# A planned graph-network kernel: the block product in two more groups, paired reciprocals, and another order of the work

## The chip, the cores and the metric

The kernel runs on one core of a Trainium2 chip. TensorE (PE) multiplies matrices and transposes, VectorE (DVE), ScalarE (ACT) and GpSimd (POOL) work on elements, and SyncE (SP) issues most transfers. All engines run side by side and wait for each other through semaphores. The metric is the device time of one execution in microseconds. Matmul results go to PSUM, which has eight banks of 128 x 512 float32; everything else is kept in SBUF. All arithmetic is float32.

## The reference

`x` is (128, 64, 256): 128 graphs of 64 nodes with 256 features; `adj` is (128, 64, 64). Four layers follow each other, each as `x = layernorm(x + layer(x, adj))`:

```python
# layer 0: gated graph network, five steps, A = (adj != 0)
for l in range(5):
    m = h @ weight[l]
    agg = einsum('bij,bid->bjd', A, m)
    h = gru_cell(agg, h, w_ih, w_hh, b_ih, b_hh)
# layer 1: graph isomorphism network, W1 is (256, 1024), W2 is (1024, 256)
agg = epsilon * x + adj @ x
h = silu(rmsnorm(agg @ W1 + b1))
out = h @ W2 + b2
# layer 2: hyperbolic: logmap0, adj @ x, expmap0, project
# layer 3: graph attention
h = x @ W_w.T + W_b
u = adj * exp(e[:, None] + f[None, :] + a_b)     # e = h @ a1, f = h @ a2
out = (u / sum(u)) @ h
```

## The kernel before

**Tiling.** Two graphs share the 128 partitions as one block, with a block-diagonal adjacency tile of 128 x 128. There are 64 blocks. Four blocks make a group (`NB` = 4, 512 rows), so there are 16 groups, numbered 0 to 15. `group(g)` records all the work of one group: loads of `x` and `adj`, five recurrent steps (`gated`), layer 0's residual and normalisation, layer 1 (`by_sums` or `as_it_is`, then the second product `ps_o`), layer 2 (`ps_sup`), layer 3 (`ps_a`, `ps_att`) and the store. Buffers are taken in three sets, by `g % 3`.

**Seven products for eight.** A product of a 2 x 2 block matrix with another needs eight block products. The kernel uses a scheme of seven (Winograd's variant of Strassen's), with sums of the weights' blocks made once at the start and sums of the activations' blocks made by DVE. The recurrent products (lines 755 and 761, PSUM tiles `p_r`, `p_u`, `p_v`, `p_w`, `p_hx`, `p_ix` and so on) use it in all groups. Layer 1's first product uses it in groups 0 to 13 (`by_sums`, PSUM tiles `p_1h`, `p_uh`, `p_vh`, `p_wh`: 28 matmuls of 256 columns, ten additions on DVE at line 947). Groups 14 and 15 use `as_it_is`: 16 plain matmuls of 512 columns into `ps_hid`, with W1 loaded a second time for this.

**Normalisation.** Groups 0 to 13 (`summed`) take row sums and squares as by-products of DVE's residual addition (line 653) and of an ACT pass; groups 14 and 15 use DVE's own statistics instructions (lines 674, 675). The power -0.5 is on POOL (line 678).

**The order.** No engine's order is written out by hand. Every helper (`pe`, `dve`, `act`, `pool`, `copied` ...) only records an operation with an assumed cost; each group is one stream. `Flow.issue` then plans: it keeps a clock for each engine and time and again picks, among the next operations of up to `WINDOW` = 4 streams, the one that can start first. Ties and ranks are settled by a rule, which changes every `STRETCH` us of the plan as a digit of `CHOICES` says: 0 is the earliest stream first, 1 puts the latest stream first and transfers by stream, higher digits compare the length of the work still behind an operation, with a lag from stream to stream (`LAGS`). `copied` and `scaled` may go to ACT or DVE, as the planner finds. The operations are emitted in the planned order, and each engine executes exactly that order: an instruction whose input is late holds up everything behind it on its engine.

**Denominators.** In layer 3 a matmul per block gives 256 features and, in one more column, the denominator. DVE multiplies (line 1113), takes the reciprocal (line 1114), multiplies again (line 1115) and adds the residual (line 653), block by block.

Of the kernel before, what the change touches and what calls it, by code (L numbers as in the profile page):

```python
# [128 lines left out]
class Flow:  # L129
# [23 lines left out]
    WINDOW, STRETCH, LAGS = 4, 4.0, (60.0, 150.0)  # L153
    CHOICES = ("0001210202220220200202001001011000011111001011100001101010000011101000001000101020011100002211002111"
               "0010002212011101012212212100222012102200120001000200200012010111210112220000000202201121220010001010"
               "0101010111011100020120010000001100000000010010010020012002000010100022210001100000200000220210100100"
               "0011110100100021120110001101100200002101000000100001000011010111011010100010010010200102001101000100"
               "2011010001000100000011000010101102000012100000100020221100000001000010001100000000100102112000002011"
               "0021000010011011100111000000100100110100022111011111110001100101110110110000111000011000")
# [81 lines left out]
def kernel(  # L241
# [41 lines left out]
    NG = B // G  # L283
    NBLK = B // 2
    NF = 3
# [59 lines left out]
    x_rows = x.rearrange("(g b t) n d -> g (t n) b d", b=NB, t=2)  # L345
    out_rows = out.rearrange("(g b t) n d -> g (t n) b d", b=NB, t=2)
    adj_blocks = adj.rearrange("(g b t) i j -> g t i b j", b=NB, t=2)
# [13 lines left out]
    loads, plain = {}, []  # L361

    def load(g):
        s = g % NF
        xt = unit("B", s, f"x_{g}", (P, NB, D))
        flow.op("SP", 0.5, lambda: nc.sync.dma_start(xt.tile(), x_rows[g]), [xt], kb=512)
        for t in range(2):
            q = quads[t]
            flow.op("SP", 0.75, lambda q=q, t=t: nc.sync.dma_start(edge[s][q, :, q], adj_blocks[g, t]),
                    [(edge[s], t)], kb=64)  # L370
        loads[g] = xt
# [226 lines left out]
    def group(g):  # L598
        s = g % NF

# [4 lines left out]
        def u(tag, name, shape=(P, R)):  # L605
            return unit(tag, s, f"{name}_{g}", shape, bufs(tag))
# [7 lines left out]
        def feats_of(dst, src, n):  # L614

            ps = bank("ps_T")
            for j in range(2):
                for c in range(KD):
                    turn(lambda j=j, c=c: nc.tensor.transpose(
                        ps[:, c * HR + j * P:c * HR + (j + 1) * P], src[:, 2 * n + j, c * P:(c + 1) * P], ident.tile()),  # L620
                        [ps], [(src, 2 * n + j)])
            copied(512, lambda: dst[:, :, half(n)], lambda: blocks_of(ps.tile()), [(dst, n)], [ps])

        def rows_of(src, n):

            ps = bank("ps_hr")
            for j in range(2):
                for c in range(KD):
                    turn(lambda j=j, c=c: nc.tensor.transpose(  # L629
                        ps[:, j * D + c * P:j * D + (c + 1) * P],  # L630
                        src[:, c, (2 * n + j) * P:(2 * n + j + 1) * P], ident.tile()), [ps], [(src, n)])
            return ps

        def aggregate(dst, src, b0, n):

            ps = bank("ps_agg")
            for j in range(2):
                for c in range(KD):
                    pe(128, lambda j=j, c=c: matmul(
                        ps[:, c * HR + j * P:c * HR + (j + 1) * P], src[:, b0 + j, c * P:(c + 1) * P],  # L640
                        ed[:, 2 * n + j, :], 0, 1), [ps], [(src, b0 + j), ed])
            copied(512, lambda: dst[:, :, half(n)], lambda: blocks_of(ps.tile()), [(dst, n)], [ps])
            return ps
# [14 lines left out]
        def layer_norm(y, st, tag, name, norm=None):  # L658
# [5 lines left out]
            if summed:  # L664
                dve(4, lambda: nc.vector.tensor_scalar(mv[:, :, 0], st[:, :, 0], -1.0 / D, None, OP.mult), [mv], [st])  # L665
                for b in range(NB):
# [4 lines left out]
                    ve[:, :m, :], over(st[:, :, 1], m), 1.0 / D, eps2[:, :m, :], OP.mult, OP.add), [ve], [st])  # L671
            else:
                for b in range(NB):
# [3 lines left out]
                    ve[:, :m, :], over(mv[:, :, 1], m), eps2[:, :m, :], OP.add), [ve], [mv])  # L677
            pool(1.25, lambda: nc.gpsimd.tensor_tensor(rstd[:, :m, :], ve[:, :m, :], pow2[:, :m, :], OP.pow), [rstd], [ve])  # L678
# [12 lines left out]
        if g == NG - 2:  # L691


            for k in range(KD):
                w = unit("h", (NG - 3) % NF, f"w1_{k}", (P, H), 2)
                flow.op("SP", 0.5, lambda w=w, k=k: nc.sync.dma_start(w.tile(), w1k[:, k, :]), [w], kb=512)
                plain.append(w)
# [7 lines left out]
        copied(512, lambda: adjT.tile(), lambda ps=ps: tiles_of(ps.tile()), [adjT], [ps])  # L705
        for t in range(2):
            q = quads[t]
            dve(128, lambda q=q: nc.vector.tensor_scalar(ed[q, :, q], ed[q, :, q], 0.0, None, OP.not_equal),
# [6 lines left out]
        def gated(l, h):  # L715
# [5 lines left out]
            def agg_of(n):  # L721

                if l:
                    ps = rows_of(h, n)
                    copied(512, lambda: hr[:, 2 * n:2 * n + 2, :], lambda: blocks_of(ps.tile()),
                           [(hr, 2 * n), (hr, 2 * n + 1)], [ps])
                aggregate(agg, hr, 2 * n, n)
# [8 lines left out]
            def sums(x, i):  # L736
                t = t_of[i]
                dve(512, lambda: nc.vector.tensor_sub(t[:, :2, :], x[:, :, half(1)], blocks_of(x[:, 0, :])),  # L738
                    [(t, t1), (t, t3)], [x], True)
                dve(256, lambda: nc.vector.tensor_sub(t[:, t2, :], x[:, 1, half(1)], t[:, t1, :]),  # L740
                    [(t, t2)], [(x, 1), (t, t1)], True)
                dve(256, lambda: nc.vector.tensor_sub(t[:, t4, :], t[:, t2, :], x[:, 1, half(0)]),
# [8 lines left out]
            def gate(ps, m, v, first, last):  # L751

                for i, w in ((1, w_h), (0, w_a[l])):
                    for c in range(KD):
                        pe(256, lambda i=i, w=w, c=c: nc.tensor.matmul(  # L755
# [4 lines left out]
            def prod(ps, j, w, m, v, first=False):  # L760
                pe(256, lambda: nc.tensor.matmul(  # L761
# [3 lines left out]
            def onto(o, ps, j, x, w, r):  # L765
                dve(300, lambda: nc.vector.tensor_add(o(), ps[:, j * HR:(j + 1) * HR], x()), w, [ps, *r])

            def state_side():
# [11 lines left out]
                def biased(n, c, ps, j, x, r):  # L780
                    dve(300, lambda: nc.vector.scalar_tensor_tensor(  # L781
# [3 lines left out]
                copied(256, su, lambda: px[:, :HR], [(hs, 0)], [px])  # L785
                prod(px, 0, w_hn, m12, block(1, 0)[1])
                scaled(256, out(0, 0), lambda: px[:, :HR], lambda: 1.0, lambda: b(0), [(hnb, (0, 0))], [px, half_b])
# [17 lines left out]
            def plus(o, n, ps, x, m):  # L805
                dve(512, lambda: nc.vector.tensor_add(o[:, :, half(n)], blocks_of(ps.tile()), x[:, :, half(m)]), of(o, n), [ps, *of(x, m)])  # L806

            def tanh_half(c, o, src, i, w, r):
                act(256 if len(w) == 1 else 512, lambda: nc.scalar.activation(  # L809
                    o(), src(), AF.Tanh, bias=half_b[:, i * KD + c:i * KD + c + 1], scale=0.5), w, [*r, half_b], TANH)  # L810

            def times_state(n):
                dve(512, lambda: nc.vector.scalar_tensor_tensor(
# [3 lines left out]
            def input_side():  # L817
# [14 lines left out]
                onto(0, 1, lambda: px[:, HR:].unsqueeze(1), px)  # L832
                prod(py, 1, w_in[l], ms3, sum_of(t3)[0], True)
                prod(py, 0, w_in[l], ms1, sum_of(t1)[0])
                onto(3, 1, lambda: py[:, HR:].unsqueeze(1), py)
# [5 lines left out]
                onto(1, 2, lambda: blocks_of(py.tile()), py)  # L841
# [3 lines left out]
            copied(420, lambda: uu[:, :, half(1)], lambda: blocks_of(p1.tile()), of(uu, 1), [p1])  # L845
# [26 lines left out]
            for c in range(KD):  # L872
                act(512, lambda c=c: nc.scalar.activation(uu[:, c, :], uu[:, c, :], AF.Tanh, bias=bih(2 * KD + c)),
                    [*of(uu, 0, c), *of(uu, 1, c)], [*of(uu, 0, c), *of(uu, 1, c), cols], TANH)
            for n in range(2):
                v = half(n)
                dve(512, lambda v=v: nc.vector.tensor_sub(hN[:, :, v], h[:, :, v], uu[:, :, v]), [(hN, n)], [(h, n), *of(uu, n)], True)
                dve(512, lambda v=v: nc.vector.scalar_tensor_tensor(
                    hN[:, :, v], uz[:, :, v], 1.0, hN[:, :, v], OP.add, OP.mult), [(hN, n)], [(hN, n), *of(uz, n)], True)
                dve(512, lambda v=v: nc.vector.scalar_tensor_tensor(  # L880
# [275 lines left out]
```

## Time and profile before

| quantity | value |
|---|---|
| median of 3 runs | 2380.03 us (2379.65 to 2380.22) |
| profiled execution | 2378.74 us |
| its span, first to last instruction | 2376.8 us |
| granted TensorE clock in it | 0.994 |
| PE busy | 2329.7 us, 98% |
| weight loads (PEld) busy | 2039.0 us, 86% |
| DVE busy | 1892.0 us, 80% |
| ACT busy | 1247.2 us, 52% |
| POOL busy | 341.2 us, 14% |

The span runs from the first to the last instruction of the program; the execution's time is a little longer. PE and PEld overlap. A float32 matmul leaves two PE records in the trace. In the tables by stretch, "clock" is the share of full speed granted to TensorE. A wait "A <- B: total, times, longest" is idle time of A's engine that ended when B was done. The chain of work is followed back from the last instruction, at each step to what released it.

### The profile page before, as it was taken

Reading aid. Unit: us, or ns where it says so; the run is one execution under the profiler, and the core shown is the slowest. Engines: PE = TensorE matmul, PEld = TensorE weight load, DVE = VectorE, ACT = ScalarE, POOL = GpSimd, SP = SyncE. Lnnn points to the kernel's source line nnn. Section 1 sums busy time; section 2 is a strip of 40 time slices with the busy share of each in tenths; the row PEclk is TensorE's granted clock in tenths of the full one; section 3 lists DMA queues with packets and bytes.
Section 4 is the critical chain, followed back from the end, with each engine's and each line's share of the span. In section 5 each row is a group of like instructions: output and inputs, shape, how many; then the busy total and the mean of one; then the engine's idle time right before and its main releaser. Section 6 shows DMA issues by size and latency. Waiting matters only on the chain.

```text
span 2376.8 us, 32667 instructions
## 1 busy us (share of the span) xinstructions
PE 2329.7 (98%) x11938; PEld 2039.0 (86%) x11938; DVE 1892.0 (80%) x4293; ACT 1247.2 (52%) x2667; POOL 341.2 (14%) x272
## 2 busy tenths in 40 slices
PE   9999999999999999999999999999999999999995
PEld 8788888888888888888888888888888888888864
DVE  5688878878878878888787787878798787887865
ACT  3333455566445546465644655555465555545364
POOL 0300111411110200211101121201212120021011
PEclk9999999999999999999999999999999999999997
DMA  3000001000000000000000000000000000000000
GB/s 123 10 1 1 12 1 36 3 10 28 13 1 1 30 1 27 3 28 2 10 21 1 18 12 1 30 1 30 1 28 3 1 30 1 27 1 10 27 10 18
DMA packets 39729, 36.22 MB, mean 15 GB/s; under 512 B 9957, under 2 KB 38657, under 8 KB 39569
## 3 DMA queue, kind: packets, MB, share of 16 engines
q1 hardware_dynamic: 37840, 32.25, 4.3%
q8 instruction: 95, 1.56, 0.3%
q10 hardware_dynamic: 1328, 1.31, 0.2%
q0 software_dynamic: 400, 0.57, 0.1%
q14 instruction: 66, 0.53, 0.1%
HBM read 25.74 MB, written 8.39 MB: 14 GB/s over the span
## 4 chain that ended last, share of the span: by engine, by line
PE 93%; DVE 5%; ACT 1%; issue 1%; POOL 0%; POOLq 0%; ACTq 0%; DVEq 0%
PE p_v L755 11%; PE p_r L755 11%; PE p_w L755 11%; PE ps_o L313 9%; PE ps_agg L313 7%; PE p_hy L761 6%; PE p_u L755 6%; PE p_iy L761 6%; PE p_hx L761 4%; PE p_ix L761 4%; PE ps_hr L629 3%; PE ps_a L313 2%; PE p_vh L942 2%; PE p_wh L942 2%; PE p_1h L942 2%; PE ps_sup L313 1%
## 5 line engine op out<-in xcount | busy, mean ns | idle before, releaser
L678 POOL TENSOR_TENSOR rstd<-ve,pow 128x4 f32<-128x4 f32 (+1 forms) x64 | 78.9, 1233 | 1309.1 <-DVE ve L670 1192.2
L313 PE MATMUL ps_o<-w2s,hid 128*128 128x256 f32 x1024 | 230.9, 381 | 0.0
L313 PEld LDWEIGHTS ps_o<-w2s,hid 128*128 128x128 f32 x1024 | 194.7, 191 | 26.3
L755 PE MATMUL p_v<-tB,w_a 128*128 128x256 f32 x640 | 170.9, 380 | 0.0
L755 PE MATMUL p_v<-tA,w_h 128*128 128x256 f32 x640 | 170.3, 380 | 0.0
L755 PE MATMUL p_r<-hT,w_h 128*128 128x256 f32 x640 | 168.3, 381 | 0.0
L755 PE MATMUL p_r<-agg,w_a 128*128 128x256 f32 x640 | 167.3, 379 | 0.0
L809 ACT ACTIVATE U<-U,half_b 128x512 f32<-128x512 f32 (+1 forms) x160 | 95.2, 629 | 106.8 <-DVE U L806 106.7
L313 PEld LDWEIGHTS ps_agg<-edge,hr 128*128 128x128 f32 x1024 | 137.4, 192 | 7.9 <-issue 0.5
L313 PE MATMUL ps_agg<-edge,hr 128*128 128x128 f32 x1024 | 138.9, 275 | 0.0
L761 PE MATMUL p_iy<-tB,w_in 128*128 128x256 f32 x480 | 133.7, 380 | 0.6 <-DVE V L826 0.5
L755 PEld LDWEIGHTS p_v<-tB,w_a 128*128 128x128 f32 x640 | 120.7, 190 | 15.9
L755 PEld LDWEIGHTS p_r<-agg,w_a 128*128 128x128 f32 x640 | 120.0, 190 | 16.4 <-issue 1.0
L761 PE MATMUL p_hy<-tA,w_hn 128*128 128x256 f32 x480 | 132.1, 380 | 1.9 <-DVE tA L738 1.1
L781 DVE SCALAR_TENSOR_TENSOR hnb<-p_hy,half_b,hs 128x256 f32<-128x256 f32 x240 | 108.7, 478 | 31.6 <-PE p_hy L761 30.4
L331 ACT COPY agg<-ps_agg 128x512 f32<-128x512 f32 x148 | 86.0, 582 | 90.0 <-PE ps_agg L313 89.2
L755 PEld LDWEIGHTS p_v<-tA,w_h 128*128 128x128 f32 x640 | 119.1, 190 | 16.0 <-DVE U L806 0.8
L809 ACT ACTIVATE V<-V,half_b 128x256 f32<-128x256 f32 (+1 forms) x160 | 88.1, 586 | 76.6 <-DVE V L806 76.2
L331 ACT COPY hr<-ps_hr 128x512 f32<-128x512 f32 x122 | 70.8, 583 | 106.7 <-PE ps_hr L629 105.5
L755 PEld LDWEIGHTS p_r<-hT,w_h 128*128 128x128 f32 x640 | 114.6, 190 | 13.9 <-ACT V L331 0.4
L667 ACT ACTIVATE x_n<-y,mv 128x256 f32<-128x256 f32 x168 | 83.3, 498 | 58.8 <-DVE mv L665 58.7
L336 ACT ACTIVATE x_n<-y,off,rstd 128x256 f32<-128x256 f32 x160 | 84.0, 589 | 42.6 <-DVE off L682 42.6
(262 smaller groups left out, 5825.7 us busy)
## 6 DMA issues: line engine op xcount, KB each, us to landing
x<-in_x_dram SPq DMA_DIRECT2D x16, 512.0 KB, 3.5
xr<-in_x_dram SPq DMA_DIRECT2D x16, 512.0 KB, 3.5
out_dram<-x_n SPq DMA_DIRECT2D x16, 512.0 KB, 2.9
edge<-in_adj_dram SPq DMA_DIRECT2D x32, 64.0 KB, 2.3
wm<-in_L_gnn_weight_dram SPq DMA_DIRECT2D x5, 256.0 KB, 4.8
w2s<-in_L_gnn_W_dram SPq DMA_DIRECT2D x1, 1024.0 KB, 9.4
w<-in_L_gnn_W_dram SPq DMA_DIRECT2D x2, 512.0 KB, 3.4
w_in_L_gnn_w_hh_dram<-in_L_gnn_w_hh_dram ACTq DMA_DIRECT2D x1, 512.0 KB, 5.4
```

The lines of the kernel that those rows point to most:

```text
L313: return nc.tensor.matmul(o, lhsT, rhs, start=(k == 0), stop=(k == nk - 1))
L331: flow.either([("ACT", 0.22 + 0.00077 * n, lambda: nc.scalar.copy(o(), i())), ("DVE", 0.145 + 0.00105 * n, lambda: nc.vector.tensor_copy(o ...
L336: flow.either([("ACT", 0.3 + 0.0008 * n, lambda: nc.scalar.activation(o(), i(), AF.Identity, bias=bias(), scale=scale())), ("DVE", 0.145 + ...
L629: turn(lambda j=j, c=c: nc.tensor.transpose(ps[:, j * D + c * P:j * D + (c + 1) * P], src[:, c, (2 * n + j) * P:(2 * n + j + 1) * P], iden ...
L667: act(400, lambda b=b: nc.scalar.activation(o[:, b, :], y[:, b, :], AF.Square, bias=mv[:, b, 0:1], accum_out=st[:, b, 1:2]), [(o, b), (st, ...
L678: pool(1.25, lambda: nc.gpsimd.tensor_tensor(rstd[:, :m, :], ve[:, :m, :], pow2[:, :m, :], OP.pow), [rstd], [ve])
L755: pe(256, lambda i=i, w=w, c=c: nc.tensor.matmul(ps[:, c * HR:(c + 1) * HR], w[:, m, c * P:(c + 1) * P], v[i][0](), start=first and i == 1 ...
L761: pe(256, lambda: nc.tensor.matmul(ps[:, j * HR:(j + 1) * HR], w[:, m, :], v[0](), start=first, stop=True, skip_group_check=True), [ps], [ ...
L781: dve(300, lambda: nc.vector.scalar_tensor_tensor(out(n, c)(), ps[:, j * HR:(j + 1) * HR], b(c), x(), OP.add, OP.add), [(hnb, (n, c))], [p ...
L809: act(256 if len(w) == 1 else 512, lambda: nc.scalar.activation(o(), src(), AF.Tanh, bias=half_b[:, i * KD + c:i * KD + c + 1], scale=0.5) ...
L942: pe(256, lambda c=c: nc.tensor.matmul(ps[:, c * HR:(c + 1) * HR], w1f[:, w, (2 * q + c) * P:(2 * q + c + 1) * P], v[0](), start=first and ...
```

## The change

The grouping stays at four blocks and 16 groups; a list `SIZES` now holds the group sizes, and many lines are only rewritten in terms of it (`HB`, `HR`, `R`, `feats`, `in_rows`, `halves_of`, `blocks_in`), with the same shapes as before. Four things differ in what is executed:

- `as_it_is` and its loads of W1 are gone: groups 14 and 15 take `by_sums` like the others.
- Layer 3's denominators are done for two blocks at a time: both matmuls into two banks, then one reciprocal and one product for the pair.
- The planner has another list of choices, with stretches of 6 us and one rule more (lag 0).
- Some assumed costs that the planner uses are other numbers (a copy of 512 columns out of PSUM was costed as 420 in two places, for example). They alter the plan, not an instruction.

```diff
-    WINDOW, STRETCH, LAGS = 4, 4.0, (60.0, 150.0)
-    CHOICES = ("0001210202220220200202001001011000011111001011100001101010000011101000001000101020011100002211002111"
...
+    WINDOW, STRETCH, LAGS = 4, 6.0, (0.0, 60.0, 150.0)
+    CHOICES = ("0010000320333333330030000000030000303010330000003330300030300030300003033330301303000001103313000330"
...
-        if g == NG - 2:
-            for k in range(KD):
-                w = unit("h", (NG - 3) % NF, f"w1_{k}", (P, H), 2)
-                flow.op("SP", 0.5, lambda w=w, k=k: nc.sync.dma_start(w.tile(), w1k[:, k, :]), [w], kb=512)
-                plain.append(w)
...
-        def as_it_is():
-            for c in range(KH):
-                ps, (v, parts) = bank("ps_hid"), chunk(c)
-                for k in range(KD):
-                    pe(512, lambda ps=ps, k=k, c=c: matmul(
-                        ps.tile(), plain[k][:, c * P:(c + 1) * P], aggm[:, k, :], k, KD), [ps], [plain[k], aggm])
-                copied(512, lambda v=v: v, lambda ps=ps: ps.tile(), parts, [ps])
-                square(c)
-
-        as_it_is() if plain else by_sums()
+        by_sums()
...
-        for b in range(NB):
-            ps = bank("ps_att")
-            pe(256, lambda ps=ps, b=b: matmul(ps[:, :D + 1], adjT[:, b, :], hw[:, b, :D + 1], 0, 1), [ps], [adjT, (hw, b)])
-            dve(4, lambda ps=ps, b=b: nc.vector.tensor_mul(rd[:, b:b + 1], ps[:, D:D + 1], hw[:, b, D + 1:]), [(rd, b)], [ps, (hw, b)])
-            dve(4, lambda b=b: nc.vector.reciprocal(rd[:, b:b + 1], rd[:, b:b + 1]), [(rd, b)], [(rd, b)])
-            dve(4, lambda b=b: nc.vector.tensor_mul(rd[:, b:b + 1], rd[:, b:b + 1], hw[:, b, D + 1:]), [(rd, b)], [(rd, b), (hw, b)])
-            onto_rows(y3, b, st3, ps, 0, lambda b=b: rd[:, b:b + 1], x3, [(rd, b)])
+        for b0 in range(0, NB, 2):
+            att, two = [bank("ps_att") for _ in range(2)], slice(b0, b0 + 2)
+            for j, ps in enumerate(att):
+                b = b0 + j
+                pe(256, lambda ps=ps, b=b: matmul(ps[:, :D + 1], adjT[:, b, :], hw[:, b, :D + 1], 0, 1), [ps], [adjT, (hw, b)])
+                dve(4, lambda ps=ps, b=b: nc.vector.tensor_mul(rd[:, b:b + 1], ps[:, D:D + 1], hw[:, b, D + 1:]), [(rd, b)], [ps, (hw, b)])
+            parts = [(rd, b0), (rd, b0 + 1)]
+            dve(4, lambda two=two: nc.vector.reciprocal(rd[:, two], rd[:, two]), parts, parts)
+            dve(4, lambda two=two: nc.vector.tensor_mul(rd[:, two], rd[:, two], hw[:, two, D + 1]), parts, [*parts, (hw, b0), (hw, b0 + 1)])
+            for j, ps in enumerate(att):
+                b = b0 + j
+                onto_rows(y3, b, st3, ps, 0, lambda b=b: rd[:, b:b + 1], x3, [(rd, b)])
```

## The prediction

> **What bounds the kernel now.** I read the page's busy times and the shares of the chain first. They name the engine.
>
> ```profile
> PE 2329.7 (98%) x11938; PEld 2039.0 (86%) x11938; DVE 1892.0 (80%) x4293; ACT 1247.2 (52%) x2667; POOL 341.2 (14%) x272
> PE 93%; DVE 5%; ACT 1%; issue 1%; POOL 0%; POOLq 0%; ACTq 0%; DVEq 0%
> ```
>
> PE (TensorE) is busy for 98% of the span and holds 93% of the chain, so the time is PE's work plus PE's gaps. VectorE (DVE) at 80% is the next limit: it causes gaps wherever it falls behind. Next, the busy time by stretches of 60 us shows where PE is not full.
>
> ```profile
> 360.00:420.00 60.00, 58.74 (x315) 51.69 (x314) 53.17 (x123) 33.21 (x78) 7.14 (x4) 1.00 0.11 36
> 420.00:480.00 60.00, 57.34 (x292) 49.09 (x291) 51.85 (x80) 35.18 (x62) 25.30 (x18) 1.00 0.01 3
> ...
> 2220.00:2280.00 60.00, 57.04 (x263) 43.56 (x261) 51.66 (x106) 27.16 (x49) 6.04 (x4) 1.00 0.06 18
> 2280.00:2340.00 60.00, 51.44 (x200) 38.19 (x200) 32.56 (x97) 33.71 (x63) 7.36 (x6) 0.91 0.00 1
> 2340.00:2400.00 60.00, 14.37 (x65) 11.48 (x64) 25.03 (x99) 16.98 (x40) 6.74 (x5) 0.82 0.05 18
> ```
>
> The columns are stretch, length, then busy time of PE, PEld, DVE, ACT and POOL, and the granted clock. PE lacks 1.3 and 2.7 us in the two early rows, and 3.0, 8.6 and 22.4 (36.8 less 14.4) us in the last three. The two rows of the start lack 3.0 us and the 35 rows between 120 and 2220 us lack 10.1 us together; 26 of the 35 show no gap. So 34 of 47 idle us lie behind 2220 us, where only groups 14 and 15 are left. The waits of PE name the causes, and the chain gives the order of that end.
>
> ```profile
> PE ps_T L619 <- ACT x_n L336: 10.0, 1, 10.0
> PE ps_sup L313 <- ACT tan L1048: 5.9, 1, 5.9
> PE p_ix L761 <- DVE V L826: 3.3, 2, 2.6
> ...
> PE ps_ss L313 <- DVE sqt L930: 2.1, 1, 2.1
> ```
>
> ```profile
> 2262.99 5.15 PE ps_hid L313 x12
> ...
> 2303.41 25.48 PE ps_o L313 x118
> ...
> 2336.52 3.58 PE ps_sup L313 x8
> ...
> 2352.20 4.21 PE ps_a L313 x16
> ```
>
> The last recurrent product ends at 2262.8 us, the last ps_o at 2328.9, the span at 2376.8. So there are 66.1 us from the first to the second, and a tail of 47.9 us behind it in which the normalisations of two groups run on DVE, ACT and POOL and PE mostly waits.
>
> **Prices.** Two records make one fp32 matmul. ps_o gives 25.48 us / 59 = 0.432 us per 256 columns; ps_hid 5.15 / 6 = 0.858 per 512. Out of the same chain: a transpose 0.11, an aggregation matmul 0.222 (8 records 0.89), a ps_ss matmul 0.20.
>
> **Layer 1's first product in groups 14 and 15.** Before: 16 matmuls of 512 columns, 13.73 us. After: 28 of 256, 12.10 us. The difference is 1.63 us, 3.3 us for both. A rule of the Trainium skill speaks against this ("TensorE: Matmul & The Clock Gate", "Back-to-back issue gap"): in a stream of weight load and matmul the spacing is set by both, 81 ns at 128 columns, some 28 ns over the bare stream, and nothing extra at 512. With 28 ns on each of the four passes of an fp32 matmul (0.858 us for 512 columns is four times 512 at 2.4 GHz), 28 matmuls would pay 3.1 us and the edit would lose 1.5 us per group, 3.0 in all. The rows decide: 0.432 is half of 0.858 within 1%, with as many weight loads beside it as here. I take -3.3.
>
> On the other engines: ten additions out of PSUM per group come to DVE, which the first fourteen groups show at 0.688 us, and three differences (0.88, 0.49, 0.49), 8.7 us per group; ACT loses four copies of 0.58. These are not free: they lie where DVE paces PE. They are counted in the walk below. The two loads of W1 (512 KB, 3.4 us to landing) and their issues leave SP's queue; no wait of PE is on them, so 0.
>
> **Denominators by pairs.** Reciprocal and product (0.163 + 0.159 us) are issued 32 times in place of 64: 10.3 us less DVE. DVE has 485 us free, so under PE's work this is worth 0; in the tail one group's share, 0.65 us, is on the chain and is counted there. The cost: the first block of a pair waits for the second's matmul (0.43 us) and two banks are held; PE at 98% shows that banks are not short.
>
> **The end in the new order.** What I can read of the changed kernel is the order of instructions on each engine, not times. Group 13 is now held back: 24 of its 32 ps_o matmuls, and its layers 2 and 3, stand behind the last recurrent product. PE's work behind that point:
> before: 32 ps_hid 27.5, 8 transposes 0.9, 8 aggregations 1.8, ss 1.6, rms 0.9, 64 ps_o 27.6, 8 sup 3.5, 16 ps_T 1.8, 16 ps_a 7.0, 8 att 3.5 = 76.1 us;
> after: 24 ps_o 10.4, transposes 0.9, 16 aggregations 3.6, 56 products 24.2, ss 1.6, rms 0.9, 64 ps_o 27.6, 12 sup 5.2, 24 ps_T 2.6, 24 ps_a 10.4, 12 att 5.2 = 92.6 us.
> So 16.5 us move behind the point, and with the 3.3 saved, 19.8 us less lie ahead of it. The wait of 2.65 us at 2259 us (p_ix behind the state additions L826, because DVE does group statistics first) also goes: in the new order the additions of group 14 are interleaved with the other group's rows.
>
> How long does the new end take? I walk the listed orders with the rows' durations from the last recurrent product (0).
> (a) DVE ends group 14's state (4 x 0.7) between group 15's rows and its statistics (4 x 0.5), POOL's pow 1.1, ACT's x_n: first aggregation at 13.5, where PE has 11.2 us of work: 2.3 idle. Copies and the late x_n of group 14 cost about 1 more.
> (b) Products: DVE has some 24 us queued (20 additions of 0.69, six differences, 15 small ones of 0.17 for group 13, sums of squares 0.77). The squares of group 15 are summed at 39.5, PE got to 38.4. ss, ms, pow 1.16, rms, first product of DVE (0.74) and Silu with a table load (1.28 + 0.72): ps_o of group 15 starts at 48.4, idle 1.9.
> (c) 32 ps_o take 13.8; group 14's squares and rms come late by about 1 and 0.7; its ps_o starts at 64.8 and ends, with 33 matmuls left (14.3), at about 80. Idle in all about 9 against 6 before.
> (d) The tail. Tan of group 14 is ready after 7.7 (before: 7.6). Then three groups share DVE: from there on its list sums to 34.9 us (y 0.48 each, statistics 0.5 a block, small ones 0.17, two additions of wb 1.14). Two places queue: th of group 15 and 14 behind one Tanh table load (1.28), and the second half copy of group 14's x3T on ACT behind four squares of group 13 (2.8), which wait for DVE. The chain reaches the last att at 39.5, pow at 43.3, x_n at 44.7, and with the 4.3 us from last x_n to span end (2372.5 to 2376.8) I get 49. Before: 47.9.
> So the end takes 80 + 49 = 129 us against 114.0 before.
>
> Clock: behind idle stretches of 5.9 and 10.0 us the records of ps_sup and ps_a last 0.427 in place of 0.216 (clock 0.82 in the last row), about 3.6 us in all. The skill's rule (same page, "What's actually happening") is half clock after an idle window of about 3.4 us. The longest idle of the walk between two tail products is about 4.4, so by the rule the half clock can return: 129 would be 132. By the row it need not: the wait of 2.65 us at 2259 was followed by full speed. I take 129 and keep 132 in the range.
>
> **The body under a new order.** Start (3.0) and the gaps from 120 to 2220 us (10.1) depend on a planned order that cannot be timed from a listing. Below: 10.1 us less, all gone. Above: each of the 35 rows has the mean gap of the nine that show one (10.1 / 9 = 1.1), 39 us, 29 more. Nearest is the row itself, since the same work runs at the same DVE load: 0.
>
> **Sum.** 2262.8 - 19.8 - 2.7 + 129 = 2369.3 us of span, 7.5 less than 2376.8. The profiled execution took 2378.74, 1.9 more than its span; the median of the runs shown is 2380.03, 3.2 more than the span. Prediction 2369.3 + 3.2 = 2372.5, rounded 2372.
>
> **Rivals.**
> 1. The gain is eaten (within 0.2%). The DVE queue of three groups makes the tail 55 instead of 49: 2378. For it: DVE is the chain there and ACT waits behind it. Against: PE's idle tail has room.
> 2. Slower: the tighter order opens gaps in the body. Every PE instruction there waits in a fixed order for DVE, as p_ix and p_hy do now; in the recurrent stretches from 120 to 300 us DVE is at 81 to 85%. It decides for slower by 0.2% once body gaps pass 10.1 + 12.3 = 22.4 us, 0.64 per row of 60 us; at 0.8 per row the time is 2390. Against: 26 rows show none.
> 3. Clearly faster: the order closes the body's gaps and the waits of (a) to (c), 10.1 + 4: 2358. For it: the gaps are few and large, and one other order may miss all of them. Against: DVE's load in (b).
> 4. The product's saving doesn't appear, by the rule above: 3.0 lost in place of 3.3 saved, 2378.
>
> **How the numbers follow.** Forecast 0.5, rival 1 and 4 together 0.2, rival 2 0.1, rival 3 0.2. A measurement of this kernel tells about 0.2%, 4.8 us, from no change: faster means below 2375.3, slower above 2384.8. The forecast's own range, 2366 to 2378, lies four fifths below 2375.3: with rival 3 that makes 0.6, and as part of rivals 1 and 4 ends just below the bound, 0.68. Slower keeps 0.09, the rest is same. Range 2357 to 2382: it takes in rivals 1, 3 and 4 and the 3 us of half clock, and leaves rival 2 out.
>
> **What would show it.** p_1h to p_wh in the last two groups at 0.432 us each and no ps_hid; 32 reciprocals; 110 to 135 us from the last p_iy to the end with group 13's ps_att among the last products; the tail from the last ps_o at 46 to 53; idle PE between 120 and 2220 us of 5 to 15 us. The prediction is wrong if the body's idle time changes by more than 8 us, or if the tail, with DVE over 70% busy in it, is not near 49.

## The result and the profile after

The changed kernel takes 2366.73 us (median of 4 runs, 2364.33 to 2366.86) against 2379.84 us (2379.32 to 2380.22): ratio 0.9943, 95% interval 0.9925 to 0.9960, 13.1 us less. The profiled execution took 2366.68 us with a span of 2364.9 us; before it was 2378.74 and 2376.8. So the spans differ by 11.9 us.

Busy times and the shares of the chain, kernel after:

```profile
PE 2329.6 (99%) x11986; PEld 2046.1 (87%) x11986; DVE 1904.2 (81%) x4271; ACT 1236.0 (52%) x2643; POOL 340.1 (14%) x272
PE 91%; DVE 7%; ACT 1%; issue 1%; POOL 0%; POOLq 0%; ACTq 0%; DVEq 0%
```

PE is still the bound, and its busy time is the same within 0.1 us although its work is 3.3 us smaller by the prices of the prediction. So the 11.9 us are idle time. Busy time by stretches says where; the first two rows answer to the early rows shown of before, the others to its last three:

```profile
360.00:420.00 60.00, 60.00 (x302) 52.76 (x302) 46.55 (x116) 31.80 (x69) 8.92 (x7) 1.00 0.00 1
420.00:480.00 60.00, 60.00 (x321) 53.50 (x320) 49.10 (x104) 31.31 (x67) 4.61 (x3) 1.00 0.08 27
...
2220.00:2280.00 60.00, 55.57 (x282) 48.25 (x281) 53.84 (x125) 29.52 (x61) 9.88 (x6) 1.00 0.03 10
2280.00:2340.00 60.00, 49.38 (x211) 39.26 (x210) 45.41 (x151) 38.91 (x88) 11.61 (x9) 0.85 0.00 1
2340.00:2400.00 60.00, 13.59 (x54) 9.92 (x52) 16.00 (x72) 15.56 (x40) 4.03 (x4) 0.89 0.07 26
```

The same view, cut at the points of the prediction's walk (last recurrent product at 2234.4 us, last ps_o at 2313.4 us):

```profile
0.00:120.00 120.00, 116.66 (x576) 96.22 (x577) 79.61 (x175) 40.70 (x91) 27.56 (x48) 1.00 0.21 66
120.00:2220.00 2100.00, 2094.44 (x10870) 1852.42 (x10869) 1709.38 (x3752) 1111.33 (x2363) 287.01 (x205) 1.00 0.04 12
2220.00:2234.40 14.40, 14.40 (x72) 12.70 (x71) 13.16 (x26) 2.24 (x4) 0.00 (x0) 1.00 0.00 0
2234.40:2313.40 79.00, 73.32 (x362) 62.44 (x362) 68.19 (x182) 51.43 (x103) 14.54 (x10) 1.00 0.02 8
2313.40:2364.90 51.50, 30.81 (x112) 22.29 (x111) 33.89 (x139) 30.31 (x82) 10.98 (x9) 0.72 0.09 31
```

Length less PE's busy time is the idle time of a stretch. The same cut of before (at 2262.8 and 2328.9 us) gives the left column:

| idle time of PE, us | before | after |
|---|---|---|
| 0 to 120 | 3.0 | 3.3 |
| 120 to 2220 | 10.1 | 5.6 |
| 2220 to the last recurrent product | 2.7 | 0.0 |
| from there to the last ps_o | 2.9 | 5.7 |
| tail | 28.3 | 20.7 |
| sum | 47.0 | 35.3 |

The waits of PE, kernel after (total, times, longest):

```profile
PE ps_att L313 <- ACT hw L1098: 4.5, 2, 3.2
PE p_1h L949 <- ACT hid L331: 3.3, 2, 2.0
PE ps_T L634 <- ACT x_n L336: 3.0, 1, 3.0
PE ps_sup L313 <- ACT tan L1046: 2.9, 1, 2.9
```

The one wait of 10.0 us for x_n is now 3.0 and the one of 5.9 for tan is 2.9: group 13's layers 2 and 3 stand in these holes. What they leave is at a lower clock. Timeline of PE in the tail, kernel after (start, length, instruction, idle before it and its releaser):

```profile
2313.22 1.89 PE L313 MATMUL ps_sup<-tan,adjT 128*128 128x256 f32 x8
...
2316.33 3.75 PE L313 MATMUL ps_a<-wattT,x3T 128*128 128x258 f32 x16 [0.35 <-DVE x3T L332]
2322.94 3.78 PE L313 MATMUL ps_sup<-tan,adjT 128*128 128x256 f32 x8 [2.85 <-ACT tan L1046]
2329.92 3.79 PE L313 MATMUL ps_att<-hw,adjT 128*128 128x257 f32 x8 [3.20 <-ACT hw L1098]
2336.69 2.17 PE L634 MATMUL ps_T<-ident,x_n 128*128 128x128 f32 x8 [2.98 <-ACT x_n L336]
2338.65 5.75 PE L313 MATMUL ps_a<-wattT,x3T 128*128 128x258 f32 x16
```

The same eight records of ps_sup take 1.89 us at 2313 and 3.78 at 2323; 16 records of ps_a take 3.75 at 2316 and 5.75 at 2339. Half clock costs PE here up to 1.9 + 1.9 + 1.1 + 2.0 = 6.9 us (ps_sup, ps_att, ps_T and ps_a). Before, it cost more than the 3.6 of the prediction: ten records of ps_o, 2.3 us at full clock, took 4.0 behind a wait of 2.10 us (timeline of PE, kernel before):

```profile
2297.97 1.16 PE L313 MATMUL ps_ss<-ones,sqt 128*128 128x1 f32 x8 [2.10 <-DVE sqt L930]
2299.00 3.98 PE L313 MATMUL ps_o<-w2s,hid 128*128 128x256 f32 x10
```

That makes about 5.2 us before, so half clock takes back some half of the 3.3 us of work that PE saved. What takes back the other half is not shown. Not all of the 6.9 us is on the path: this is asked below.

### The profile page after: what moved, and what is told of

Same layout as the page of the kernel before. It is cut to its first block, busy times and chain, and to the rows that moved or that the text cites. A ratio compares the mean times of both kernels' runs of the same rounds, so it can differ in the third digit from the quotient of the medians.

```text
span 2364.9 us, 32771 instructions
## 1 busy us (share of the span) xinstructions
PE 2329.6 (99%) x11986; PEld 2046.1 (87%) x11986; DVE 1904.2 (81%) x4271; ACT 1236.0 (52%) x2643; POOL 340.1 (14%) x272
## 4 chain that ended last, share of the span: by engine, by line
PE 91%; DVE 7%; ACT 1%; issue 1%; POOL 0%; POOLq 0%; ACTq 0%; DVEq 0%
PE p_r L762 11%; PE p_w L762 11%; PE p_v L762 11%; PE ps_o L313 9%; PE ps_agg L313 7%; PE p_hy L768 6%; PE p_u L762 6%; PE p_iy L768 5%; PE p_hx L768 4%; PE p_ix L768 4%; PE ps_hr L644 3%; PE ps_a L313 2%; PE p_vh L949 2%; PE p_wh L949 2%; PE p_1h L949 2%; PE ps_sup L313 1%
## 5 line engine op out<-in xcount | busy, mean ns | idle before, releaser
L1000 ACT ACTIVATE hid<-hid,cols 128x512 f32<-128x512 f32 x128 | 85.9, 716 | 76.6 <-DVE hid L998 76.5
```

Of the source, the lines that this page charges most:

```text
L1000: act(R, lambda v=v, c=c: nc.scalar.activation(v, v, AF.Silu, scale=rmsc(c)), parts, [*parts, cols], SILU)
```

## The experiments

The theory to be tested was: the 13 us are PE's work (3.3 us), a fuller body, and an end in which group 13 fills the holes. The rival: one of the parts alone does it, and the others do nothing or harm. "Fitted" means here that the list of choices was searched for the very operations and costs that are recorded. In all twelve runs the matmuls, copies and normalisations are as in the one or the other kernel, save where an edit or an expectation says otherwise.

**The product alone.** The kernel before, with `by_sums` in groups 14 and 15, without the two loads of W1, and with its old list of choices, filled up with 0.

```diff
...
-        as_it_is() if plain else by_sums()
+        by_sums()
```

> The kernel before with one edit: groups 14 and 15 take the seven block products; the list of choices is the old one, and PE's listed order is the same as before up to the second last aggregation of layer 1, then differs. Theory A (the product is worth its 3.3 us of PE work wherever it stands): 2376.6 us. Rival B (the ten additions per group on DVE, 0.69 us each, stand in front of the sums of squares, which PE waits for, and eat the saving): 2379 to 2384 us, with more idle PE between the last recurrent product and ps_o than the 6 us of before.

Measured: 2402.04 us, ratio 1.0091 (1.0077 to 1.0104), 22 us slower than before and beyond both theories. PE's order is that of before up to 2261.9 us (11614 of its 11938 records). The body has the same idle time as before (2089.89 us busy between 120 and 2220 us, against 2089.88). All of the loss is in the end. Waits of PE:

```profile
PE ps_T L620 <- ACT x_n L337: 11.1, 1, 11.1
PE ps_sup L314 <- ACT tan L1042: 10.4, 2, 7.1
PE p_vh L936 <- DVE hid L941: 8.4, 3, 4.9
```

p_vh waits for the scheme's own additions on DVE, as the prediction feared ("they lie where DVE paces PE"), and the two waits of the tail are longer than before. The span is 24.7 us longer: 16.6 us are idle time, and 8.1 us are PE's busy time, which grew although its work is 3.3 us smaller. So PE spends 11.4 us more on its records than the work explains, most of it at half clock (granted clock 0.987 in place of 0.994). In the old order the product is not a gain of 3.3 us but a loss of 22.

**The order alone, and the changed kernel with the old order.** First the kernel before with the new list, stretch and lags; then the changed kernel with the old ones. In the first, the last eight digits and all behind them are 3; the second list is filled up with 0.

```diff
-    WINDOW, STRETCH, LAGS = 4, 4.0, (60.0, 150.0)
-    CHOICES = ("00012102022202202002020010010110...
...
+    WINDOW, STRETCH, LAGS = 4, 6.0, (0.0, 60.0, 150.0)
+    CHOICES = ("00100003203333333300300000000300...
...
```

> The kernel before with the new list of choices, stretches of 6 us and three lags; plain products in groups 14 and 15, reciprocals block by block. The last 48 us of the list are set to the lag of 60 us. Theory A (order is worth some 10 us: 5 in the body, 3 at the last state, the rest in the end): 2367 to 2373 us, with idle PE of 4 to 8 us in the rows from 120 to 2220 us. Rival C (the list only fits the plan that it was searched on; any other recorded work makes it a chance order): 2376 to 2390 us, with more than 10 us idle in those rows.

> The changed kernel with the old list of choices, stretches and lags; product and pairs stay. Theory A: product and pairs without the order give 2374 to 2378 us. Rival B (they are worth nothing): 2379 to 2384 us. Rival C (a list that doesn't fit its plan opens gaps): above 2384 us, with more than 15 us of idle PE in the rows from 120 to 2220 us.

Measured: 2580.08 us (ratio 1.0841, 1.0827 to 1.0856) and 2644.47 us (1.1106, 1.1091 to 1.1121). This is far more than I had reckoned with. Waits of PE of the first:

```profile
PE ps_hr L628 <- DVE hT L879: 46.7, 17, 7.6
PE p_iy L760 <- DVE U L825: 19.1, 8, 5.4
```

and of the second:

```profile
PE ps_hr L647 <- DVE hT L890: 46.9, 18, 6.8
PE ps_T L637 <- ACT x_n L339: 28.3, 5, 10.6
PE p_iy L771 <- DVE U L836: 19.1, 8, 5.4
```

Between 120 and 2220 us PE is busy for 2002.9 and 1978.2 us, so 97 and 122 us idle, spread over the recurrent steps. A digit of the list speaks of a moment of the plan, not of an operation: with other recorded operations or assumed costs the same digit falls on other choices, and once the plan differs, what the rest of the list does is arbitrary; this is how I read it, no run shows it pick by pick. So neither run tells what the new order is worth. They tell that each list is worth something only with the recording that it was searched for, and what the lack of fit costs here: 200 us against the kernel before, 278 against the changed one.

**The pairs undone.** The changed kernel in its order, with a reciprocal and a product per block.

```diff
-            dve(4, lambda two=two: nc.vector.reciprocal(rd[:, two], rd[:, two]), parts, parts)
+            dve(4, lambda b0=b0: [nc.vector.reciprocal(rd[:, b:b + 1], rd[:, b:b + 1]) for b in (b0, b0 + 1)], parts, parts)
...
```

> The changed kernel in its own order on every engine; only each pair's reciprocal and product are issued as two instructions per block, at the same place. Theory A: 2 pairs of the last group on the chain, two more instructions each of 0.17 to 0.2 us: 0.7 us longer, 2367.4 us, and 10.3 us more DVE busy time that costs nothing elsewhere. Rival (DVE at 81% is so near its limit that 10 us of small instructions show in the body): 2370 us or more.

Measured: 2365.55 us (2364.25 to 2366.34), ratio 0.9937 (0.9924 to 0.9949), against 2366.73 with pairs. Undoing the pairs costs nothing that can be measured, so neither number of the expectation came. 64 more small instructions moved DVE's busy time from 1904.2 to 1904.6 us, not by 10.3: the second of two starts while the first still runs. Two single reciprocals take 0.23 us together here (at 2340.41 us), and the one over two blocks took 0.17 in the changed kernel (at 2341.17). Both matmuls of a pair still stand ahead of the small instructions, so the number of instructions is tested here, not the order block by block of before.

**A shared prefix with a dull end, with the product and without.** To take the arbitrary list out of the comparison, both kernels of this pair keep the new order up to a point, and from there on all digits are 0. The second has plain products and the two loads of W1 in groups 14 and 15.

```diff
-               "3000000111310003100100311030000003300111101111202220010111101102112122201121121202122111000")
+               "3000000111310003100100311030000003300111101111202220010111101102100000000000000000000000000000000000"
+               "0000000000000000000000000000000")
```

> The changed kernel; only the last 26 digits of its list (156 us of the plan) are 0, earliest group first. PE's listed order is that of the changed kernel over 3360 of 3526 rows. Theory C (the searched digits carry the time, place by place): the body's idle time stays (about 5 us in the rows from 120 to 2220), the end grows, 2380 to 2410 us. Rival (the end is bound by its own chain whatever the order): 2364 to 2370 us.

> As the run with the last 26 digits 0, but with plain products in groups 14 and 15 (and their loads of W1). PE's order is the same as in that run up to row 3432. Theory A (the seven products are worth 3.3 us of PE work where the order is not fitted to either): 2 to 5 us longer than that run. Rival B (the additions on DVE cost what PE saves): the same within 2 us, or shorter.

Measured: 2415.86 us (ratio 1.0150, 1.0137 to 1.0164) with the product, 2403.12 us (1.0094, 1.0079 to 1.0109) without: the first above its range, the second as rival B had it. Two things follow. The last 26 digits alone are worth 49 us to the changed kernel. And in an end that nobody searched, the seven products are 12.7 us slower than the plain ones. PE's waits with the product:

```profile
PE ps_T L635 <- ACT x_n L337: 17.2, 2, 9.7
...
PE ps_rms L995 <- POOL rms L992: 7.1, 2, 5.8
```

and with plain products, where ps_T waits once:

```profile
PE ps_T L635 <- ACT x_n L337: 9.7, 1, 9.7
```

The longer waits are for x_n and rms, which come behind DVE's work. That the scheme's additions make them late is the likely reading; shown is it only for p_vh, in the first experiment.

**Both fitted.** The fair comparison: the changed kernel with plain products and with seven, both keeping the digits of the first 2040 us, both with the rest of the list searched anew with the same number of tries. A search by the plan's own end time doesn't promise the best order for either, but both had the same chance.

```diff
-               "3000000111310003100100311030000003300111101111202220010111101102112122201121121202122111000")
+               "3000000111310003100100311030000003300111231123002310032121011133300310113222331331131220000000000000"
+               "0000000000000000000000000000000000")
...
-        by_sums()
+        as_it_is() if plain else by_sums()
```

> The changed kernel with plain products (and their two loads of W1) in groups 14 and 15, as before, and the choices behind 2040 us of the plan searched anew for it; up to there PE's order is the changed kernel's. Unlike the earlier run with plain products, the order fits the work that is recorded. Theory A (the product saves 3.3 us of PE's work and relieves nothing else, so fitted for fitted it is worth 3 to 7 us, and the rest of the change's 13 us comes from the order of the first 2200 us): 2371 to 2378 us, 3 to 7 above the run below. Theory B (the whole gain is the order's, and the product's additions on DVE take back what PE saves): within 2 us of the run below, or faster than it.

> The changed kernel (seven products in groups 14 and 15) with the choices behind 2040 us of the plan searched anew, with as many tries as in the run above. Theory A: 2366 to 2372 us, 3 to 7 below the run above. Theory B: within 2 us of the run above, or slower than it. Idle time of PE between 120 and 2020 us as in the changed kernel, about 5 us, by both, in both runs.

Measured: 2370.53 us (2368.66 to 2370.88), ratio 0.9958 (0.9945 to 0.9970), with plain products; 2364.63 us (2363.77 to 2366.12), ratio 0.9936 (0.9924 to 0.9949), with seven. The runs of the two don't overlap; the medians differ by 5.9 us, as theory A had it, and theory B falls. Both times lie below theory A's ranges, and its second half, the rest of the 13 us in the first 2200 us, did not come: that part gave 4.5. The page's busy times and the body's row of the plain one:

```profile
PE 2329.2 (98%) x11938; PEld 2036.1 (86%) x11938; DVE 1892.0 (80%) x4258; ACT 1238.1 (52%) x2641; POOL 340.8 (14%) x272
120.00:2040.00 1920.00, 1914.42 (x9934) 1692.50 (x9933) 1558.71 (x3476) 1032.63 (x2212) 273.65 (x195) 1.00 0.04 12
```

and of the one with seven products:

```profile
PE 2326.9 (98%) x11986; PEld 2045.3 (87%) x11986; DVE 1904.9 (81%) x4279; ACT 1233.7 (52%) x2635; POOL 343.0 (15%) x272
120.00:2040.00 1920.00, 1914.41 (x9933) 1692.25 (x9932) 1558.42 (x3476) 1032.63 (x2212) 273.67 (x195) 1.00 0.04 12
```

The bodies are equal to 0.01 us: 5.6 us idle, where the kernel before has 10.1 (1909.9 us busy) in the same stretch. The spans, 2366.8 and 2362.8 us, differ by 4.0 us, of which 2.3 are PE's busy time (records at half clock included) and 1.7 idle time. So the gain of this pair can be split. With plain products, 9.5 us (2379.98 less 2370.53): 4.5 of these are the body's gaps, and the other 5 are left for the end's order. The product adds 5.9 with an end that is fitted to it. That is 15.4 us with this end, and 13.1 with the end of the change. The 4.5 are read from the rows; the 5 and the 5.9 rest on one search for each side. How much a search matters is seen at the changed kernel: the same work takes 2366.73 us with its own end and 2364.63 with the end found here.

**POOL's additions in four pieces.** The chain after showed small DVE instructions of 1.5 to 2.3 us in the end of the kernel, while POOL adds 128x1024 elements. In the last three groups POOL adds block by block; the sums are the same.

```diff
...
-        pool_sum(NB * D, lambda: xb.tile(), lambda: x1.tile(), lambda: over(b2_r.tile(), NB), [xb], [x1, b2_r])
+        pool_blocks(xb, x1, b2_r)
...
```

> The changed kernel in its own order on every engine; in groups 13 to 15 each of POOL's additions over 128 x 1024 elements (x_n plus b, x_n plus wb) is issued as four over 128 x 256. Theory P (an SBUF addition on POOL holds off DVE's SBUF instructions until it ends; in the end three small ones of DVE, L679, L1022 and L1024, last 1.5, 2.3 and 2.1 us in place of 0.17): they last at most 0.8 us, and the time falls by 2 to 4 us, 2363 to 2365. Rival (the chain goes through ACT or PE next to them anyway): 2366 to 2367 us with the three rows shorter.

Measured: 2363.66 us (2362.10 to 2364.19), ratio 0.9930 (0.9918 to 0.9942), 3.1 us below the changed kernel. Timeline of the stall in the changed kernel:

```profile
2318.11 2.35 POOL L343 TENSOR_TENSOR x_n<-x_n,wb_r 128x1024 f32<-128x1024 f32 x1
2318.20 0.18 DVE L1023 RECIPROCAL fac<-fac 128x4 f32<-128x4 f32 x1
2318.42 2.07 DVE L1024 SCALAR_TENSOR_TENSOR fac<-n,fac 128x4 f32<-128x4 f32 x1
...
2320.79 0.95 DVE L1034 SCALAR_TENSOR_TENSOR ser<-ser,n 128x4 f32<-128x4 f32 x5
...
2322.38 0.51 ACT L1046 ACTIVATE tan<-x_n,fac 128x256 f32<-128x256 f32 x1 [1.65 <-DVE n L1063]
```

and the same place with four pieces:

```profile
2316.78 2.78 POOL L631 TENSOR_TENSOR x_n<-x_n,wb_r 128x256 f32<-128x256 f32 x4
2316.88 0.18 DVE L1031 RECIPROCAL fac<-fac 128x4 f32<-128x4 f32 x1
2317.09 0.44 DVE L1032 SCALAR_TENSOR_TENSOR fac<-n,fac 128x4 f32<-128x4 f32 x1
...
2318.25 1.92 DVE L1042 SCALAR_TENSOR_TENSOR ser<-ser,n 128x4 f32<-128x4 f32 x5
...
2320.81 0.51 ACT L1054 ACTIVATE tan<-x_n,fac 128x256 f32<-128x256 f32 x1 [2.42 <-DVE n L1071]
2321.37 1.99 PE L313 MATMUL ps_sup<-tan,adjT 128*128 128x256 f32 x8 [2.61 <-ACT tan L1054]
...
2335.29 4.51 PE L313 MATMUL ps_a<-wattT,x3T 128*128 128x258 f32 x16
```

The reciprocal, with one input from SBUF, takes its 0.18 us beside POOL. L1024 has two such inputs; it begins 0.31 us after POOL and ends with it, at 2320.49 against 2320.46. The Trainium skill ("SBUF — State Buffer", "Who interferes with whom") says just this: a VectorE instruction with two SBUF inputs and a GpSimd instruction that reads SBUF exclude each other for the whole of the one that came first. Here ACT's tan, and PE's ps_sup behind it, waited for L1024.

Cutting the addition shortens L1024 but hardly this chain. In four pieces DVE gets in between two of them, and then its next instructions with two SBUF inputs are held by the later pieces: the five of L1042 take 1.92 us, where the same five (L1034) took 0.95. From POOL's start to tan it is 4.27 us in one piece and 4.03 in four, a gain of 0.24. More comes from two earlier places, ahead of layer 1's products: L679 (a TENSOR_SCALAR with one SBUF input, so two inputs are not the whole of it) falls from 1.53 to 0.59 us and L1022 from 2.32 to 0.72, PE's waits of p_1h for hid fall from 3.3 to 1.9 us, and the last ps_o ends 1.3 us earlier. These places explain 1.6 of the 4.6 us by which the spans of the two profiled executions differ. The other 3.0 are half clock that did not come: ps_sup at 1.99 us lets ps_att start 1.8 us earlier, and ps_a at 4.51 gives 1.2. Whether the pieces brought the fuller clock is not shown. So of the 3.1 us between the medians, 1.6 are shown to be POOL's.

**PE kept busy in the tail.** Transposes of the identity, read by nobody, stand on PE where it would wait. In the first of these kernels there are 24 behind group 13's ps_a, 30 ahead of its ps_att and 30 behind.

```diff
...
+                    *spun(ps, 30 if (g, b) == (NG - 3, 0) else 0),
                     matmul(ps[:, :D + 1], adjT[:, b, :], hw[:, b, :D + 1], 0, 1),
+                    *spun(ps, 30 if (g, b) == (NG - 3, NB - 1) else 0)], [ps], [adjT, (hw, b)])
```

> The changed kernel in its own order; in the tail PE also does 84 transposes of the identity into unused columns of ps_a and ps_att (24 ahead of the last ps_sup, 30 on either side of group 13's ps_att), work that nobody reads. Theory W (PE's half clock behind the idle stretches of 2.9 to 3.4 us is on the chain: ps_sup 3.8 us in place of 1.9, ps_T and ps_a 7.7 in place of 4.4): records at 0.216 us there, 3 to 5 us less, 2362 to 2364 us. Rival (the tail waits for DVE and ACT, so PE's speed is hidden): 2366 to 2368 us.

Measured: 2365.85 us (2365.34 to 2368.91), ratio 0.9942 (0.9930 to 0.9955): no gain that can be measured, although ps_sup now takes 1.99 us, ps_T 1.04 and ps_a 3.75. On the chain stands

```profile
2329.69 3.49 PE ps_att L602 x30
2333.18 1.74 PE ps_att L313 x8
```

The 30 transposes ahead of ps_att stand in its bank. They waited with it for ACT (3.21 us) and then held it up for 3.3 us: from ps_sup to ps_T the profiled execution takes 13.5 us, where it was 13.7. From the first ps_sup of the tail to the end it is 48.8 us in place of 51.7. But 1.4 us are lost ahead of that, where the edit changes nothing: behind p_1h's wait of 1.96 us, the clock granted between 2252.1 and 2256.5 us is 0.61, and after the same wait (1.99) it was 1.00 in the changed kernel. So the transposes were moved: 24 behind group 13's ps_a, 26 behind group 14's ps_sup (the expectation below says group 13's) in the bank of that ps_a, and 30 behind group 13's last ps_att.

```diff
...
+                    *(spun(held[NG - 3, NB - 1], 26) if (g, b) == (NG - 2, NB - 1) else [])], [sup[h]], [adjT, (tan, b)])
```

> The changed kernel in its own order with idle time of PE in the tail filled by transposes of the identity whose output nobody reads: 24 behind group 13's first half of ps_a, 26 behind group 13's ps_sup, 30 behind group 13's... first ps_att products, each into a bank that is already held, so that none of them waits for ACT. In the earlier run with such transposes 30 of them waited for hw and put 3.3 us on the chain. Theory W (half clock in the tail is on the chain and costs 2 to 5 us): 2361 to 2364 us, ps_sup, ps_T and ps_a of the tail at full speed (8 records of ps_a in 1.8 us or less). Rival (DVE and ACT pace the tail, and PE's half clock hides behind them): 2365 to 2367 us with those records at full speed.

Measured: 2364.34 us (2363.24 to 2365.61), ratio 0.9934 (0.9922 to 0.9947), between the two theories and nearer to theory W: 2.4 us below the changed kernel's median, while the runs of the two overlap. Timeline of PE in it:

```profile
2321.94 2.78 PE L604 MATMUL ps_a<-ident 128*128 128x128 f32 x24
2324.96 1.99 PE L313 MATMUL ps_sup<-tan,adjT 128*128 128x256 f32 x8 [0.24 <-ACT tan L1055]
2326.79 3.00 PE L604 MATMUL ps_a<-ident 128*128 128x128 f32 x26
2330.15 2.68 PE L313 MATMUL ps_att<-hw,adjT 128*128 128x257 f32 x8 [0.36 <-ACT hw L1109]
...
2338.85 3.75 PE L313 MATMUL ps_a<-wattT,x3T 128*128 128x258 f32 x16
```

Of the 6.9 us of half clock, then, 3.8 lay on the path. From ps_sup to ps_att it is 5.2 us in place of 7.0, and from ps_a to the next ps_att 3.6 in place of 5.6; the rest hid behind DVE and ACT. The profiled execution is only 1.8 us shorter, since it reaches the tail 2.0 us later: 0.6 are lost ahead of the last recurrent product, and 1.4 again behind p_1h (a wait of 1.98 us, then a clock of 0.61).

**Both.** The pieces on POOL and the moved transposes.

> Both edits: POOL's additions of 128x1024 in the last three groups in four pieces, as in the earlier run (3.1 us less than the changed kernel), and the transposes of the run above. If the two costs lie one behind the other on the chain they add: 2358 to 2361 us. If the tail is paced by DVE and ACT whatever PE's clock: 2363 to 2364 us, as with the split alone.

Measured: 2361.57 us (2361.40 to 2363.46), ratio 0.9924 (0.9910 to 0.9938). The two gains, 3.1 and 2.4 us, would give 2361.2 if they add fully, so by the medians they add. It is the fastest kernel here, 18.4 us below the kernel before, and its longest run (2363.46) is below the changed kernel's shortest (2364.33). One thing is left: in its profiled execution, the longest, the 16 records of ps_a take 5.44 us again (clock 0.68), with no wait longer than 0.83 us shortly ahead of them. Why is open.

## Why the prediction was right, and where it was off

The forecast was 2372.5, rounded 2372; the time is 2366.7, inside the range and inside the likeliest case's own (2366 to 2378). Its sum of 2369.3 us of span is 2240.3 + 129; the trace has 2234.4 + 130.5 = 2364.9. That it comes so near is in part luck: the body and the work ahead of the point were put 5.9 us too long, and half clock in the tail, put at nothing, gave 3.8 back.

- **The product's price, -3.3.** Right. Products of layer 1 stand on the chain at 1.73 us for eight records, 0.432 for each matmul of two records. The back-to-back rule that the prediction weighed would have made them slower, and no row shows that. But 3.3 is only PE's share; with a fitted end the product saves 5.9 us (4.0 by the spans), and without one it costs 12.7 to 22. That the ten additions on DVE "are not free" was right, and their sign depends on the order.
- **The wait of 2.65 us at 2259.** Gone: from 2220 us to the last recurrent product PE idles 0.0 us.
- **The body under a new order, taken as 0.** This is the term that was mis-sized: it is -4.5 us (10.1 to 5.6 us idle), the largest part of the miss of 4.4. The argument "same work at the same DVE load" only held for the order of size. The mechanism was that of rival 3, at a third of its size; the two early gaps of 1.3 and 2.7 us closed altogether. With this -4.5 and the 0.3 more at the start the first part would be 2236.1 where it is 2234.4; the other 1.7 us are busy time: PE has 21.5 us less of it ahead of the point, where 19.8 were reckoned.
- **(a) to (c), 80 us.** 79.0. Idle there was put at 9 against 6, three more than before; by the stretches it went from 2.9 to 5.7, which is 2.8 more. So both idle times were read 3 us too high, and the 80 came out because the work was put 2.3 too low (71 where 73.3 are busy).
- **(d), the tail, 49 us.** 51.5, of which 3.8 is half clock on the path (by the run that takes it away). Without it the tail would be 47.7, and the walk 1.3 us too long. DVE is busy for 33.9 us of it, near the 34.9 of the walk's list, but that is 66%, not over 70.
- **Clock.** I kept half clock at 3 us in the range but took none, since a wait of 2.65 us had been followed by full speed. This row was no ground for it: the same trace has half clock behind a wait of 2.10 us (ps_o at 2299 us, above), and in the run of the product alone the wait of 2.65 us, in the same order of instructions, is followed by a clock of 0.59. The term should have been priced; it measured 3.8 us.
- **Pairs, 0.65 us in the tail and 10.3 us of DVE.** Not to be seen: undone, the time is not longer and DVE's busy time 0.4 us more, since two small instructions in a row overlap.
- **Rivals.** Rival 1 (the tail at 55) and rival 4 (no saving) did not come. Rival 2's mechanism is real, but not in this order: it takes an order that doesn't belong to the recorded work, and then it costs 200 us and more, not 10.

What I could not know from a listing is what the runs with plain and with seven products show: that the order has the larger part of the gain (9.5 of 15.4 us in the fitted pair, with one search on each side), and that the product was a loss under both orders not made for it. Why the new list closes just these gaps of the body isn't settled: no run changed the body alone and kept the fit.

## What to carry to other kernels

When a kernel's order is planned from assumed costs and a fitted list of choices, an edit and its order can only be judged together: the same edit was worth +22, +12.7 and -5.9 us under an old, a dull and a fitted end. So search the order anew for both sides of a comparison, with equal effort. In a tail, where small instructions on three engines pass a result on, look for two things that the busy times don't show: a small VectorE instruction that lasts until a GpSimd instruction ends, and TensorE records that last twice as long after a wait of two or three microseconds. Before an edit gets the credit for the whole difference, compare the two traces piece by piece: here 3.0 of the 4.6 us between two of them were clock. Work that fills such waits must not itself wait for the engine that it is to bridge.

## What was not expected of the hardware

- A 128x1024 addition on POOL (2.35 us) kept a 128x4 DVE instruction of 0.16 us for 2.07 us, while a reciprocal beside it took its 0.18. In four pieces of about 0.7 us the same instruction took 0.44, but those behind it were held in turn, and the chain became 0.24 us shorter.
- PE's half clock cannot be told from the length of the wait alone, between 2 and 3.2 us. The clock granted just behind the wait:

| execution and place | wait, us | granted clock |
|---|---|---|
| before, p_ix at 2259.1 us | 2.65 | 1.00 |
| product alone, the same place | 2.65 | 0.59 |
| before, ps_ss at 2298.0 | 2.10 | 0.66 |
| changed kernel, p_1h at 2252.0 | 1.99 | 1.00 |
| transposes moved, the same place | 1.98 | 0.61 |
| changed kernel, ps_sup at 2322.9 | 2.85 | 0.50 |
| POOL in pieces, the same place | 2.61 | 1.00 |
| PE kept busy, transposes at 2329.7 | 3.21 | 1.00 |

Where two rows have the same place, PE's order up to it is the same in both. The Trainium skill ("TensorE: Matmul & The Clock Gate", "What's actually happening") gives an idle window of about 3.4 us; half clock came after shorter waits here, so a wait under that figure is not safe. What decides is open. It also moves the time of one and the same kernel: of the four executions of the changed one, three of 2366.68 to 2366.86 us have a granted clock of 0.994 to 0.996, the fourth, 2364.33 us, has 0.997.
